# Attention on one core: five eighths of each step's exponentials are kept and exchanged in one round, and V is applied in the step that makes them

## The chip, the core and the metric

The kernel runs on one core of a Trainium2 chip. A core has five engines that run side by side, each through its own list of instructions in order: PE multiplies matrices and writes to PSUM (eight banks of 512 f32 columns in each of 128 partitions), DVE works on vectors, ACT computes functions such as exp, POOL works on vectors too but does not reach PSUM, and SP issues DMA transfers. Sixteen DMA engines move data between HBM and SBUF, and within SBUF. The metric is the time on the device in microseconds; lower is better. All times below without a unit are microseconds, lengths of single instructions excepted where ns is given.

## What is computed

Eight sequences of 512 tokens with 512 features go through one layer of attention with 16 heads of 32. The queries and keys get a second, per-sequence term from `cond`, and the input is added to the result. Cut to what matters:

```python
Q, K, V = (split_heads(x @ W.T + b) for W, b in ((Wq, bq), (Wk, bk), (Wv, bv)))
cQ = Q + split_heads(cond @ Wq.T + bq)
cK = K + split_heads(cond @ Wk.T + bk)
attn = softmax(cQ @ cK.T / sqrt(32))
return x + (attn @ V)
```

Everything is f32.

## The kernel before

**Tasks and steps.** A task `t` is one sequence and one group of four heads: 8 sequences times 4 groups make `T` = 32 tasks. 512 queries and 512 keys are cut into four chunks of 128 each. A step `t` of the main loop (line 1086) mixes the work of several tasks so that every engine has something to do. It has four items, `i` = 0 to 3. Each item holds row scores for one query chunk of task t+1 (in the last item, of t+2), and either a third of a product that makes q, k or v of the next sequence ("P"), or the application of V ("V"). Some items start with a burst of scores as well. The products go by a scheme with seven block products instead of eight (`product`, line 446): a "first" part with 28 matmuls and an "other" part with 28.

**Row scores** (`row_max`, line 578). PE computes for each of the four heads 128 queries against 512 keys (`row_scores`, L607), queries on partitions. DVE takes each row's maximum with its sign turned (`one_max`, L574, for one head; `row_max_of`, L616, for two in neighbouring banks). ACT then computes exp(score - maximum) of the whole row and its sum in one instruction (`denominators`, L654). In most tasks, those in `KEPT` = 2 to 27, the exponentials of the first two query chunks are kept in SBUF; of the other two only the sums are used and the exponentials are written back to PSUM and lost.

**Why an exchange.** To apply V, keys have to be on the partitions. DVE can transpose blocks of 32 by 32 (`turn_kept`, L626: four instructions per task with 1,024 elements per partition each). What is left is to swap whole blocks between the four bands of 32 partitions. `swap_kept` (L640) does this in place with 18 DMA transfers of 128 KB: `move` 0 copies six blocks aside, `move` 1 copies six across, both on SP's queue; `move` 2, on POOL's queue in item 2 of the next step, copies the six from aside. Three rooms for kept exponentials rotate, and V is applied to task t-1 in step t (line 1123 or 1126).

**Bursts.** For the query chunks that are not kept the scores are computed a second time with keys on partitions (`exponentials_of_rest`, line 721): a bf16 matmul over three rows puts the maxima, split into three bf16 parts and transposed by DMA (`split_max` on POOL, `turn_max` L680 on SP), into PSUM (L727); the scores are added (L738); ACT takes exp (L748). There are two bursts of 256 queries per kept step, in items 2 and 3. Tasks outside `KEPT` recompute all 512 (L706, L709, L719).

**Applying V** (`weighted`, line 817). 16 matmuls on the exponentials of the burst, four small ones that spread the sums (L804), 16 on the kept ones (L769). DVE takes reciprocals (L814) and transposes the result (L840), POOL multiplies (L841) and adds the input (L842), and SP stores it in four pieces (L845).

**Making q, k, v.** The "first" parts go from PSUM by two ACT copies (L520, L521) and two POOL additions (L523, L524). The "other" parts of q and k go by three DVE instructions (`other_products`: L536, L481 twice), those of v by two ACT copies (L559, L560) and three POOL additions (`other_by_others`: L561 to L563).

**PSUM.** `order` keeps the eight banks in the order in which they come free; `begin` hands an item eight or (without a burst, "alone") four of them for its row scores, `released` puts them back.

**The order of work** is written out by hand: the program order of each engine is the order of the calls. `TURNED` says after which item's row scores the transposes of the next task stand. After the loop comes a tail for the last tasks (from line 1208), where V is applied in parts between crossed scores of two tasks (`part_of`, `crossed`).

Of the kernel before, what the change touches and what calls it, by code (L numbers as in the profile page):

```python
# [17 lines left out]
def kernel(  # L18
# [14 lines left out]

# [14 lines left out]
    KEPT = range(2, T - 4)  # L71
    KQ = NS // 2
# [5 lines left out]
    qkp = ctx.enter_context(tc.tile_pool(name="qkp", bufs=3))  # L78
    op = ctx.enter_context(tc.tile_pool(name="op", bufs=2))
# [124 lines left out]
    store = EB.tile([P, 18, 2, S], F32, tag="eb", name="store")  # L204

    def room(t):

        at = (t - KEPT[0]) % 3 * 4
        return store[:, at : at + 4].rearrange("p g c (h s) -> p g c h s", s=P)

    ring_at = [0]

    def chunk():

        ring_at[0] += 1
        return store[:, 8 + (ring_at[0] - 1) % 10]

    early = store[:, :8].rearrange("p c i s -> p (c i) s")
# [172 lines left out]
    def pair_of(t, n):  # L391

        if (n, t // 2) not in pairs:
            pairs[n, t // 2] = qkp.tile([P, 2, S], F32, tag=n, name=f"{n}T_{t // 2}")
        return pairs[n, t // 2]
# [25 lines left out]

# [52 lines left out]

    def plus(n, b, u, g, o, pt, rest):

        if n == "v":
            nc.vector.tensor_tensor(o, pt, rest, ALU.add)
        else:
            add = tok[:, "qk".index(n), u * 2 + g, b : b + 1]  # L480
            nc.vector.scalar_tensor_tensor(o, pt, add, rest, ALU.add, ALU.add)  # L481
# [21 lines left out]

    def first_by_others(n, b, u, dens, at, last, mixed):
# [7 lines left out]
        if mixed:  # L512
            dens((0, 1))
            nc.scalar.copy(c2, one_)
# [3 lines left out]
        else:  # L518
            dens()
            nc.scalar.copy(c2, one_)  # L520
# [5 lines left out]
    def other_products(n, b, u, dens, small, at, bias=False):  # L526
# [15 lines left out]
        if n != "v":  # L542
            for g in range(2):
                qkT[n, b * G + u * 2 + g] = pair_of(b * G + u * 2, n)[:, g, :]
# [3 lines left out]
    def other_by_others(n, b, u, dens, small, at):  # L548

        dens()  # L550
# [7 lines left out]
        m45, m23 = aside[:, 0], aside[:, 1]  # L558
        nc.scalar.copy(m45, halves(one_))  # L559
        nc.scalar.copy(m23, halves(two_))  # L560
        nc.gpsimd.tensor_tensor(c12, m45[:, 1, :], c12, ALU.add)  # L561
        nc.gpsimd.tensor_tensor(c2, m45, twice(c22), ALU.add)
        nc.gpsimd.tensor_tensor(c1, m23, c1, ALU.add)  # L563
# [14 lines left out]
    def row_max(t, qc, hold=False, w=HG):  # L578
# [14 lines left out]
        def held():  # L593
            if apart or hold and t < T - 2:
# [25 lines left out]
    kept = {}  # L620

    def turn_kept(t, n):

        pr = slice(n % NP * 2, n % NP * 2 + 2)
        e = kept[t][:, :, n // NP, pr, :].rearrange("p g h s -> p g (h s)")
        nc.vector.transpose(e, e)  # L626

    APART = [(a, g) for a in range(HG) for g in range(a + 1, HG)]
    between = store[:, 16:18]

    def swap_kept(t, move):

        def part(a, g):
            return kept[t][a * BL : (a + 1) * BL, g].rearrange("p c h s -> p (c h s)")

        for n, (a, g) in enumerate(APART):
            at = (n + 2) % HG * BL
            aside = between[at : at + BL, n // HG].rearrange("p i s -> p (i s)")
            to, of = [(aside, part(a, g)), (part(a, g), part(g, a)), (part(g, a), aside)][move]
            (nc.gpsimd if move == 2 else nc.sync).dma_start(to, of)  # L640

    def denominators(t, qc, w=HG, js=range(HG)):
# [3 lines left out]
        keep = t in KEPT and qc < KQ  # L646
        if keep and t not in kept:
            kept[t] = room(t)
        for j in js:
            of = to = banks(w + j)  # L650
            if keep:
                to = kept[t][:, :, qc, j, :].rearrange("p g (c e) -> p g c e", e=BL)
# [8 lines left out]

    def split_max(t, on=nc.gpsimd):
# [3 lines left out]
        m, sp = nmax[t], split[t % 2]  # L666
        rest = op.tile([P, NS, HG, 1], F32, tag="rest", name=f"rest_{t}")
# [7 lines left out]
    def turn_max(t):  # L675

        if t >= T:
# [3 lines left out]
            maxT[t].rearrange("p (c q) -> p c q", c=NS),  # L681
            split[t % 2].rearrange("p c h e -> p (c h e)"),
# [37 lines left out]

    def exponentials_of_rest(t, half):

        bank = [banks(i) for i in range(HG)]
        rest = slice(KQ * P, S)
        for j in range(HG):
            r = slice(j * HD, j * HD + 3)
            nc.tensor.matmul(  # L727
                bank[j],
                onesb[r, :],
                maxT[t][r, rest].unsqueeze(1).broadcast_to([3, 2, HS]),  # L730
# [3 lines left out]
        for i in range(2):  # L734
            kc = half * 2 + i
            for j in range(HG):
                r = slice(j * HD, (j + 1) * HD)
                nc.tensor.matmul(  # L738
                    bank[j][:, i * HS : (i + 1) * HS],
# [5 lines left out]
        for pr in range(NP):  # L745
            e = es[t, half, pr] = store[:, 12 + half * 2 + pr]
            for i in range(2):
                nc.scalar.activation(e[:, i, :], bank[pr * 2 + i], AF.Exp)  # L748
# [12 lines left out]
    def times_v_half(t, kc, half, pt):  # L761
        b, g = divmod(t, G)
        for j in range(HG):
            if half:
                at = kc % 2 * HS
                e = es[t, kc // 2, j // 2][:, j % 2, at : at + HS]
            else:
                e = kept[t][:, :, :, j, kc * BL : (kc + 1) * BL].rearrange("p a c e -> p c a e")
            nc.tensor.matmul(  # L769
                pt[j * HD : (j + 1) * HD, half * HS : (half + 1) * HS],  # L770
                vs[b % 2][:, kc, (g * HG + j) * HD : (g * HG + j + 1) * HD],
                e,
                start=(kc == 0),
                stop=(kc == NS - 1),
# [42 lines left out]
    def weighted(t, pt, pd, between):  # L817

        apart = masked(t)
        if t in KEPT:
            for kc in range(NS):
                times_v_half(t, kc, 1, pt)
            spread_sums(apart, pd)
            for kc in range(NS):
                times_v_half(t, kc, 0, pt)
# [7 lines left out]
        send(t, pt, rec)  # L835
# [526 lines left out]
```

## Time and profile before

| | us |
|---|---|
| Runs (median of 3) | 670.43 (669.88, 670.43, 675.13) |
| The profiled execution | 668.33 |
| Its span, first to last instruction | 666.5 |
| Mean granted clock of PE | 0.999 of full speed |

In the profile a line starts with the source line (L607 is line 607) and the engine; `psum<-kT,qT` names what is written and read; `x1024` counts records. An f32 matmul leaves two records in the trace, so `x8` stands for four matmuls. `PEld` are weight loads, which overlap PE. In a group's line the first numbers are the busy time in all and the mean length of one in ns, and behind the second bar stands how long the engine idled before them and what ended most of it. In a timeline the first number is the start, the second the length. The figure "us to landing" is from the issue of a DMA to its arrival.

### The profile page before, as it was taken

How to read it: one execution, taken by the hardware profiler on the slowest of the kernel's cores; microseconds unless marked ns; L12 is line 12 of the kernel's file. 1: busy time of each engine (PE TensorE's matmuls, PEld its weight loads, DVE VectorE, ACT ScalarE, POOL GpSimd, SP SyncE). 2: the span in 40 equal slices, each digit the busy share in tenths (PEclk: the TensorE clock that was granted, in tenths of full speed). 3: DMA queues.
4: the chain of work that ended last, by engine and by line, in shares of the span. 5: the costliest groups of instructions: out<-in, count | busy, mean ns of one | idle time of the engine just before them, and what ended most of it. 6: DMA issues, size and time to landing. Idle time of an engine off the chain costs nothing.

```text
span 666.5 us, 24514 instructions
## 1 busy us (share of the span) xinstructions
PE 659.8 (99%) x9784; PEld 339.6 (51%) x9784; DVE 561.7 (84%) x752; ACT 557.4 (84%) x1396; POOL 407.1 (61%) x577
## 2 busy tenths in 40 slices
PE   9999999999999999999999999999999999999997
PEld 8444444555555555555555555555555555555432
DVE  3798898889988888998888989888898988766877
ACT  2479889888889988888988888898888889888664
POOL 3641326677666875768566785668765776663261
PEclk9999999999999999999999999999999999999999
DMA  7723238897889888878888888787887687671111
GB/s 188 110 41 58 35 58 181 170 184 164 159 162 181 164 186 186 179 157 176 168 176 174 179 176 168 167 185 152 164 182 153 149 181 159 145 163 23 26 32 32
DMA packets 245862, 94.90 MB, mean 142 GB/s; under 512 B 229099, under 2 KB 229611, under 8 KB 245749
## 3 DMA queue, kind: packets, MB, share of 16 engines
q1 hardware_dynamic: 236500, 71.83, 56.4%
q0 software_dynamic: 7488, 20.46, 10.9%
q8 instruction: 77, 1.26, 0.8%
q10 hardware_dynamic: 1760, 1.05, 0.5%
q14 instruction: 37, 0.29, 0.2%
HBM read 19.75 MB, written 8.39 MB: 42 GB/s over the span
## 4 chain that ended last, share of the span: by engine, by line
PE 96%; DMA 1%; DVE 1%; POOL 1%; issue 0%; DVEq 0%; POOLq 0%
PE psum L456 43%; PE psum L607 19%; PE psum L769 14%; PE psum L738 6%; PE psum L753 3%; PE psum L727 2%; PE psum L709 2%; PE psum L399 2%; PE psum L706 1%; PE psum L1186 1%; PE psum L779 1%; DMA w_q<-in_L_cond_Wq_dram 1%; DMA maxT<-split 0%; PE psum L308 0%; POOL store L640 0%; PE psum L353 0%
## 5 line engine op out<-in xcount | busy, mean ns | idle before, releaser
L574 DVE TENSOR_REDUCE nmax<-psum 128x1 f32<-128x512 f32 x246 | 158.2, 685 | 71.8 <-PE psum L607 70.3
L654 ACT ACTIVATE psum<-psum,nmax 128x512 f32<-128x512 f32 x272 | 180.4, 670 | 16.6 <-DVE nmax L616 8.7
L616 DVE TENSOR_REDUCE nmax<-psum 128x2 f32<-128x1024 f32 x127 | 154.1, 1214 | 1.3 <-PE psum L607 1.3
L654 ACT ACTIVATE store<-psum,nmax 128x512 f32<-128x512 f32 x208 | 141.7, 692 | 11.4 <-DVE nmax L616 6.7
L607 PE MATMUL psum<-kT,qT 32*128 32x512 f32 x1024 | 149.7, 620 | 0.2 <-DVE kT L481 0.2
L748 ACT ACTIVATE store<-psum 128x512 f32<-128x512 f32 x208 | 107.4, 604 | 34.7 <-PE psum L738 34.7
L626 DVE STREAM_TRANSPOSE store<-store 128x1024 f32<-128x1024 f32 x104 | 127.5, 1226 | 0.0
L769 PE MATMUL psum<-store,v 128*32 128x256 f32 x1664 | 96.8, 381 | 0.0
L640 POOL DMA_DIRECT2D store<-store x156 | 77.5, 501 | 27.5 <-DMA store<-store 13.7
L769 PEld LDWEIGHTS psum<-store,v 128*32 128x32 f32 x1664 | 48.9, 110 | 46.5 <-ACT store L654 16.7
L607 PEld LDWEIGHTS psum<-kT,qT 32*128 32x128 f32 x1024 | 51.0, 183 | 39.4 <-issue 23.0
L841 POOL TENSOR_TENSOR res<-res,recs 128x512 f32<-128x512 f32 x30 | 31.4, 1048 | 42.3 <-DVE res L840 42.3
L654 ACT ACTIVATION_READ_ACCUMULATOR psum<-psum,nmax 128x1 f32 x272 | 57.1, 210 | 0.0
L738 PE MATMUL psum<-qT,kT 32*128 32x256 f32 x832 | 53.7, 374 | 0.0
L201 POOL TENSOR_TENSOR xr<-xr,bvs 128x512 f32<-128x512 f32 x30 | 38.5, 1285 | 15.1 <-DMA xr<-in_x_dram 15.0
L456 PE MATMUL psum<-wc_v,xc 128*32 128x256 f32 x768 | 47.7, 379 | 0.0
L719 ACT ACTIVATE store<-psum 128x512 f32<-128x512 f32 x72 | 37.2, 605 | 12.2 <-PE psum L709 9.0
L456 PE MATMUL psum<-xc,wc_q 128*32 128x256 f32 x720 | 44.5, 379 | 0.0
L456 PE MATMUL psum<-xc,wc_k 128*32 128x256 f32 x720 | 44.5, 379 | 0.0
L654 ACT ACTIVATION_READ_ACCUMULATOR store<-psum,nmax 128x1 f32 x208 | 43.1, 207 | 0.0
L738 PEld LDWEIGHTS psum<-qT,kT 32*128 32x128 f32 x832 | 40.8, 184 | 3.3
L842 POOL TENSOR_TENSOR res<-res,xr 128x512 f32<-128x512 f32 x30 | 38.5, 1285 | 2.4
(193 smaller groups left out, 1017.7 us busy)
## 6 DMA issues: line engine op xcount, KB each, us to landing
store<-store SPq DMA_DIRECT2D x312, 128.0 KB, 2.3
store<-store POOLq DMA_DIRECT2D x156, 128.0 KB, 3.6
out_dram<-res SPq DMA_DIRECT2D x122, 64.0 KB, 3.8
xr<-in_x_dram SPq DMA_DIRECT2D x120, 64.0 KB, 2.6
x<-in_x_dram SPq DMA_DIRECT2D x112, 64.0 KB, 2.9
w_q<-in_L_cond_Wq_dram SPq DMA_DIRECT2D x4, 256.0 KB, 3.8
w_v<-in_L_cond_Wv_dram SPq DMA_DIRECT2D x16, 64.0 KB, 2.6
w_k<-in_L_cond_Wk_dram SPq DMA_DIRECT2D x16, 48.0 KB, 2.5
```

Of the source, the lines that this page charges most:

```text
L201: nc.gpsimd.tensor_tensor(xr[t], xr[t], bias, ALU.add)
L456: nc.tensor.matmul(pt[r], still[:, r], moving, start=(kc == kcs[0]), stop=(kc == kcs[-1]))
L574: nc.vector.tensor_reduce(nmax[t][:, qc, j : j + 1, 0], pt, AX.X, ALU.max, negate=True)
L607: nc.tensor.matmul(pt, qkT["q", t][r, qc * P : (qc + 1) * P], qkT["k", t][r, :], start=True, stop=True,)
L616: nc.vector.tensor_reduce(nmax[t][:, qc, pr * 2 : pr * 2 + 2, 0], pt, AX.X, ALU.max, negate=True)
L626: nc.vector.transpose(e, e)
L640: (nc.gpsimd if move == 2 else nc.sync).dma_start(to, of)
L654: nc.scalar.activation(to, of, AF.Exp, bias=nmax[t][:, qc, j, :], accum_out=sums[t][:, qc, j, :],)
L738: nc.tensor.matmul(bank[j][:, i * HS : (i + 1) * HS], qkT["k", t][r, kc * P : (kc + 1) * P], qkT["q", t][r, rest], start=False, stop=(i == 1),
L748: nc.scalar.activation(e[:, i, :], bank[pr * 2 + i], AF.Exp)
L769: nc.tensor.matmul(pt[j * HD : (j + 1) * HD, half * HS : (half + 1) * HS], vs[b % 2][:, kc, (g * HG + j) * HD : (g * HG + j + 1) * HD], e, ...
L842: nc.gpsimd.tensor_tensor(y, y, xr.pop(t), ALU.add)
```

## The change

1. **More is kept.** Of a kept task's exponentials, query chunks 0 and 1 are kept for all keys and chunk 2 for key chunks 0 and 1 (`FULL`, `HALF`): five eighths. So the burst for key chunks 0 and 1 covers only query chunk 3 (128 queries), the one for key chunks 2 and 3 covers 256 as before. The bursts stand in items 0 (the narrow one) and 2. The row chunks are taken in the order 1, 3, 2, 0 (`IN_TURN`), because chunk 2 is written in full and chunk 0 then covers its surplus. Only the maxima of chunks 2 and 3 are split and transposed. `KEPT` reaches to 28.
2. **One round.** `meet` copies all 16 blocks (160 KB each, those that stay in their band too) from the task's room (two rooms now) into a room of its own, `MET`: 12 transfers on SP in item 0, four on POOL in item 1. `swap_kept` is gone. A fifth `turn_kept` per task is needed (`UNITS`); of the five one or more stand in the step in which they are exchanged.
3. **V in the same step.** A kept step's items are "P", "P", "P", "V", and `weighted` works on task t itself. It writes two banks, so the result is transposed in two halves; POOL's multiplication and addition and the stores follow in the next step, after `meet` (`unsent`). Step 1 applies V twice, to tasks 0 and 1, and the tail no longer applies V to task 28.
4. **Work moves from DVE to ACT and POOL.** The "other" parts of q and k go by one ACT copy, one DVE addition of the bias and three POOL additions; the "first" parts of q and k leave by a copy and a copy with bias of half the size each, and a full copy. The "other" part of v of the second half goes by DVE. In item 1 of a kept step the row maxima are four single reductions.

```diff
-    KEPT = range(2, T - 4)
-    KQ = NS // 2
+    KEPT = range(2, T - 3)
+    FULL = 2
+    HALF = 2
+    IN_TURN = (1, 3, HALF, 0)
...
-    store = EB.tile([P, 18, 2, S], F32, tag="eb", name="store")
+    PAD = HS
+    BLOCK = FULL * S + HS
+    ROOM = HG * BLOCK
+    ROOMS = (0, ROOM + PAD)
+    REST = 2 * (ROOM + PAD)
+    MET = REST + 6 * S
+    store = EB.tile([P, MET + ROOM], F32, tag="eb", name="store")
...
+    UNITS = [(S, 0), (S, 1), (FULL * S, None), (0, 0), (0, 1)]
...
+    def meet(t, ns, queue):
+        for n in ns:
+            a, g = n % HG, (n + n // HG) % HG
+            of, to = room(t) + g * BLOCK, MET + a * BLOCK
+            queue.dma_start(
+                store[g * BL : (g + 1) * BL, to : to + BLOCK],
+                store[a * BL : (a + 1) * BL, of : of + BLOCK],
+            )
...
+    def rest_at(kc):
+        return slice((FULL if kc >= HALF else FULL + 1) * P, S)
+
     def exponentials_of_rest(t, half):
+        kcs = [(2, 3), (0, 1)][half]
+        rest = rest_at(kcs[0])
+        n = S - rest.start
...
-            for kc in range(NS):
-                times_v_half(t, kc, 1, pt)
+            for kc in (2, 3, 0, 1):
+                times_v_rest(t, kc, pt[1], kc == 2, False)
             spread_sums(apart, pd)
             for kc in range(NS):
-                times_v_half(t, kc, 0, pt)
+                times_v_kept(t, kc, pt[0], range(FULL), kc == 0, kc == NS - 1)
+            for kc in range(HALF):
+                times_v_kept(t, kc, pt[1], [FULL], False, kc == HALF - 1)
...
-        return [(s, i - 2)] if i >= 2 else []
+        return [(s, 1 - i // 2)] if i % 2 == 0 else []
...
+    OTHERS = "kq"
+    MEET = (range(12), range(12, 16))
+    TURNED = {(0, 0): 1, (0, 1): 1, (2, 0): 1, (2, 1): 1, (2, 2): 1}
+    TURNED_1 = {(0, 0): 1, (0, 1): 2, (2, 0): 1, (3, 1): 1}
...
-        items = "PVPP" if t - 1 in KEPT else "VPPP"
+        items = ["P", "P", "P", "V"] if t in KEPT else ["V", "P", "P", "PV"]
...
+            if t in KEPT and i == 0:
+                while todo[t]:
+                    turn_kept(t, len(UNITS) - todo[t])
+                    todo[t] -= 1
+                meet(t, MEET[0], nc.sync)
+            while unsent:
+                unsent.pop()()
+            if t in KEPT and i == 1:
+                meet(t, MEET[1], nc.gpsimd)
+            if i == (1 if t + 1 in KEPT else 2):
                 split_max(t + 1)
                 turn_max(t + 1)
```

More of the change, by code (lines that the diff above doesn't have):

```diff
@@ L645, in denominators @@
             return
-        keep = t in KEPT and qc < KQ
-        if keep and t not in kept:
-            kept[t] = room(t)
+        keep = t in KEPT and qc <= FULL
         for j in js:
@@ L651, in denominators @@
             if keep:
-                to = kept[t][:, :, qc, j, :].rearrange("p g (c e) -> p g c e", e=BL)
+                to = of_room(room(t), qc, j, range(NS))
                 of = of.rearrange("p (c g e) -> p g c e", g=HG, e=BL)
@@ L733, in exponentials_of_rest @@
             )
-        for i in range(2):
-            kc = half * 2 + i
+        for i, kc in enumerate(kcs):
             for j in range(HG):
```

232 lines of the change are left out of this document (132 added, 100 removed).

## The prediction

> **What bounds the kernel now.** I read the busy line and the chain first, then the windows of four steps of the main loop, then PE's timeline of one step.
>
> ```profile
> span 666.5 us, 24514 instructions
> PE 659.8 (99%) x9784; PEld 339.6 (51%) x9784; DVE 561.7 (84%) x752; ACT 557.4 (84%) x1396; POOL 407.1 (61%) x577
> PE 96%; DMA 1%; DVE 1%; POOL 1%; issue 0%; DVEq 0%; POOLq 0%
> ```
>
> ```profile
> 313.36:333.09 19.73, 19.73 (x316) 10.49 (x313) 17.44 (x23) 17.23 (x45) 11.89 (x19) 1.00 0.79 164
> sum 78.27, PE 78.27 PEld 41.12 DVE 69.48 ACT 69.27 POOL 54.26; mean PE 19.57 PEld 10.28 DVE 17.37 ACT 17.32 POOL 13.56
> ```
>
> The columns are length, then busy time of PE, PEld, DVE, ACT, POOL, then granted clock, DMA share and GB/s. A step lasts 19.57 on the mean of four; PE is busy all of it, DVE 17.37, ACT 17.32, at full clock. A modelled end can hide a short wait of PE, so I take PE's costs from one start to the next:
>
> ```profile
> 313.36 0.39 PE L727 MATMUL psum<-maxT,onesb 3*128 3x512 bf16 x4
> 313.58 1.03 PE L738 MATMUL psum<-qT,kT 32*128 32x256 f32 x16
> 314.45 1.02 PE L607 MATMUL psum<-kT,qT 32*128 32x512 f32 x8
> 315.41 1.07 PE L456 MATMUL psum<-xc,wT_q 128*32 128x256 f32 x16
> ...
> 318.57 0.40 PE L727 MATMUL psum<-maxT,onesb 3*128 3x512 bf16 x4
> ...
> 329.43 1.93 PE L769 MATMUL psum<-store,v 128*32 128x256 f32 x32
> 331.19 0.23 PE L804 MATMUL psum<-apart,modulo 128*32 128x16 f32 x8
> 331.25 1.91 PE L769 MATMUL psum<-store,v 128*32 128x256 f32 x32
> 333.09 0.40 PE L727 MATMUL psum<-maxT,onesb 3*128 3x512 bf16 x4
> ```
>
> An f32 matmul is two records. A burst of recomputed scores costs 0.22 for its bf16 maxima and 0.87 for the rest: 1.09. The item around it lasts 5.21 (313.36 to 318.57). Applying V costs 3.66 (329.43 to 333.09). So the question is what the change takes from PE, and whether another engine then makes PE wait.
>
> **PE, the scores.** A kept step has two bursts of half its queries. In the changed kernel the burst for key chunks 0 and 1 covers one query chunk: 16 records of 128 columns and four bf16 matmuls of 256. If cost goes with columns it is 0.11 + 0.435 = 0.545, and 0.545 is saved. The trace has no 32-row matmul of 128 columns; the weights may be what is left, since their size does not shrink. The nearest rows:
>
> ```profile
> 661.54 0.60 PE L849 MATMUL psum<-ident,store 128*128 128x128 f32 x4
> 661.98 0.38 PE L1311 MATMUL psum<-ident,store 128*128 128x128 f32 x2
> L738 PEld LDWEIGHTS psum<-qT,kT 32*128 32x128 f32 x832 | 40.8, 184 | 3.3
> ```
>
> Four f32 loads and matmuls of 128 by 128 start 0.44 apart, 0.11 each. A row group runs four records of the narrow burst one after another: 4 x 0.11 = 0.44, as by columns. The other bound takes the load's whole 184 ns: 0.74 + 0.11 = 0.85, and 0.24 is saved. I take 0.545, by L849, which does both things in its 0.11. The Trainium skill ("TensorE: Matmul & The Clock Gate", The mechanism) says that a weight load overlaps running matmuls only where their row groups differ. With the 107 ns for 128 columns of its section LDWEIGHTS, a narrow record would take 107 + 107 ns and the burst would save 0.12, an estimate; but the wide burst's four rounds in 0.87 leave no room for such a load beside the columns, so the trace disagrees.
>
> Steps 2 to 27 gain this: 26 x 0.545 = 14.2. Step 28 becomes a kept step. It now runs from its first burst to the tail's:
>
> ```profile
> 597.24 0.40 PE L706 MATMUL psum<-maxT,onesb 3*128 3x512 bf16 x4
> ...
> 619.28 0.40 PE L706 MATMUL psum<-maxT,onesb 3*128 3x512 bf16 x4
> ```
>
> That is 22.04, against 19.57 - 0.545 = 19.0: 3.0 saved. Applying V streams as many columns as before in 80 records instead of 64; eight records of 16 columns pass in 0.06 (331.19 to 331.25), so short ones cost no more than their columns, and I count nothing.
>
> **The tail.** V of task 28 moves from the tail into the loop, and V of task 1 from step 2 into step 1: PE's 3.66 moves, and the tail gets 3.66 shorter if PE alone bounds it. But there:
>
> ```profile
> 624.52 2.06 ACT L1201 ACTIVATE store<-psum 128x512 f32<-128x512 f32 x4 [0.55 <-PE psum L1186]
> ...
> 627.71 2.06 ACT L1201 ACTIVATE store<-psum 128x512 f32<-128x512 f32 x4 [0.63 <-PE psum L1186]
> ```
>
> Each turn is 3.19, of which 2.06 are exponentials that empty the banks and about 1 is V's filler. Without it PE waits for banks. Bounds: nothing lost, 3.66 lost; I take 1.5.
>
> **DVE.** It becomes the engine next to PE:
>
> ```profile
> L574 DVE TENSOR_REDUCE nmax<-psum 128x1 f32<-128x512 f32 x246 | 158.2, 685 | 71.8 <-PE psum L607 70.3
> L616 DVE TENSOR_REDUCE nmax<-psum 128x2 f32<-128x1024 f32 x127 | 154.1, 1214 | 1.3 <-PE psum L607 1.3
> L626 DVE STREAM_TRANSPOSE store<-store 128x1024 f32<-128x1024 f32 x104 | 127.5, 1226 | 0.0
> L536 DVE TENSOR_TENSOR qT<-psum,qT 128x256 f32<-128x256 f32 x15 | 6.2, 412 | 0.0
> L481 DVE SCALAR_TENSOR_TENSOR qT<-psum,tok,qT 128x512 f32<-128x512 f32 x29 | 20.5, 740 | 0.2 <-PE psum L727 0.2
> L412 DVE TENSOR_SCALAR qT<-psum,tok 128x512 f32<-128x512 f32 x2 | 1.5, 750 | 0.8 <-PE psum L399 0.8
> ```
>
> Per step: a fifth transpose, +1.23; two single reductions for one double, 1.37 - 1.21 = +0.16; the result's transpose in two, +0.1 (bounds 0 and one more 0.7). One "other" product of q or k per step loses 0.41 + 2 x 0.74 = 1.89 and keeps one of 0.75; one V product in four steps comes back, about 1.89 / 4 = 0.47. Sum 17.37 + 1.23 + 0.16 + 0.1 - 1.89 + 0.75 + 0.47 = 18.2 of 19.0. So it fits, but unevenly. In three steps of four the item of the full burst carries two transposes behind its maxima. Its maxima start 1.09 + 1.05 into the item (L574 began 1.05 after L607 at 314.45: see DVE's rows below, 315.50), take 2.58 and end at 4.72; two transposes end at 7.2, or 2.0 into the next item, where maxima could start at 1.05. The lag is 0.95, or about 0.5 as neighbours on DVE overlap. The last two exponentials of those scores free banks for the next step's first row scores:
>
> ```profile
> 328.36 1.14 PE L607 MATMUL psum<-kT,qT 32*128 32x512 f32 x8
> L654 ACT ACTIVATE store<-psum,nmax 128x512 f32<-128x512 f32 x208 | 141.7, 692 | 11.4 <-DVE nmax L616 6.7
> ```
>
> Without lag they end at 1.05 + 2.58 + 2 x 0.69 = 5.0 in the item of V; PE asks for the banks at 4.73 (328.36 to 333.09) + 0.55 = 5.28. So the lag less 0.28, 0.2 to 0.7, may show as a wait in three steps of four, or nothing. I take the low end, 0.15 on the mean of steps: 27 x 0.15 = 4.
>
> ```profile
> 313.49 0.72 DVE L840 STREAM_TRANSPOSE res<-psum 128x512 f32<-128x512 f32 x1
> 314.13 1.20 DVE L626 STREAM_TRANSPOSE store<-store 128x1024 f32<-128x1024 f32 x1
> 315.50 0.69 DVE L574 TENSOR_REDUCE nmax<-psum 128x1 f32<-128x512 f32 x1 [0.17 <-PE psum L607]
> ```
>
> **ACT and POOL** stay below PE. ACT loses half of four rest exponentials (604 ns each to about 400: -0.8) and gains about 0.5 in copies of q and k: near 17. POOL drops two DMA issues of 0.49 and gains three additions for each "other" product of q and k, less one V product in four steps:
>
> ```profile
> L748 ACT ACTIVATE store<-psum 128x512 f32<-128x512 f32 x208 | 107.4, 604 | 34.7 <-PE psum L738 34.7
> L494 ACT COPY v<-psum 128x256 f32<-128x256 f32 x2 | 0.8, 407 | 0.0
> L523 POOL TENSOR_TENSOR qT<-qT 128x512 f32<-128x512 f32 x13 | 16.7, 1285 | 9.6 <-ACT qT L521 9.6
> L524 POOL TENSOR_TENSOR qT<-qT 128x256 f32<-128x256 f32 x14 | 10.2, 732 | 4.6 <-DVE qT L516 3.6
> ```
>
> 13.56 - 0.98 + 3.30 - 0.82 = 15.1 of 19.0. If that cover went, k would reach the next batch's row scores late; at an item's distance it does not.
>
> **The exchange.** It used to have almost a step; now V waits for it in its own step.
>
> ```profile
> 307.43 8.65 SPq L640 DMA_DIRECT2D store<-store  x12
> L640 SPq DMA_DIRECT2D store<-store x312: 507/545/1876, 91.1 to 587.0; - x156
> DMA to landing us min/median/max: 2.1/3.1/5.8
> maxT<-split SPq DMA_TRANSPOSE x29, 3.4
> ```
>
> The fifth transpose stands first in the next step, so the transfers may start about 2.0 after the previous V ended (L626 above: 314.13 + 1.20, V having ended at 313.36). SP issues twelve in 6.5 (545 ns each) to 8.65; the last lands 2.3 to 5.8 later: at 10.8 to 16.5. POOL's four stand behind its additions for that item's product, which ends near 4.7: some 2.0 of additions and 2.0 of issues bring the last to 9 to 10, landed by 16. The kept part of V starts 19.0 - 2.3 = 16.7 after the previous V. So it is covered, by 0.2 at the worst pairing. Behind the twelve on SP stand four result stores and the transposed maxima that the next narrow burst needs: 10.65 + 4 x 0.65 + 3.4 = 16.7, before 19.0. Each transfer is a quarter larger; if that lengthens the issue too, 8.65 x 1.25 = 10.8, and the maxima land at 18.8. If the cover is gone, PE waits by what is missing, each step.
>
> **Sum.** 668.33, the profiled execution, of which 666.5 is the span: 668.33 - 14.2 - 3.0 + 1.5 + 4 = 656.6. The median of the runs lies 2.1 above (670.43, runs 669.88 to 675.13): 658.7.
>
> **The rivals.**
> Weights bound the narrow burst: it saves 0.24 and not 0.545, 26 x 0.305 = 8 more, 667. For it: the 184 ns in each load's row. Against: L849.
> DVE becomes the bound, and the kernel slower. Its maxima wait for PE (70.3 of 71.8 idle in L574's row), its result transposes for V's end, and both stand in line before the transposes. Now it idles 19.57 - 17.37 = 2.2 per step. If that idle stays, a step is 18.2 + 2.2 = 20.4: 26 x 0.83 = 22 more, less 1.6 in step 28, plus 1.5: median 692. It decides from an idle of 1.4 on (19.57 - 18.2). At 0.8 it costs nothing. Against: much of the idle was waiting that work can fill.
> The exchange comes late: at 5.8 for each last landing and one more issue delay of 2, V waits 1.8 a step: +48, median 703. Against: the landings have a median of 3.1.
> PE gains without any wait, and the tail fully: 668.33 - 17.2 + 2.1 = 653.2; this is the low end of my forecast.
>
> **Chances.** PE-bound with small waits, 652 to 664: 0.66. Weights: 0.10. DVE: 0.13, half of it at partial idle, 664 to 678. Exchange: 0.05. The rest, 0.06, is what the rows don't show, such as strided transposes or exponentials that cost more. A range of 651 to 676 leaves about 2 in 10 out. About 1% is what a measurement can tell from no change: faster, below 663.7, takes the forecast and little else, 0.67; within, 0.17; slower, above 677.1, 0.16.
>
> **What would show it.** Right: V-end to V-end about 19.0 to 19.2, narrow burst near 0.55, DVE busy 18.2, transfers landed before V's kept part. Wrong: PE waiting for DVE or ACT at the row scores, a narrow burst of 0.85, or V idle for a transfer.

## The result and the profile after

The changed kernel takes 694.96 us (median of 4 runs, 692.08 to 696.87), the kernel before 671.83 in the same comparison: a ratio of 1.034 [1.028, 1.040], so 3.4% slower where 2% faster was forecast. The profiled execution took 696.87, its span is 695.0.

The page of the changed kernel: span, busy line, chain by engine and by line.

```profile
span 695.0 us, 25350 instructions
PE 653.9 (94%) x10240; PEld 355.0 (51%) x10240; DVE 583.4 (84%) x798; ACT 535.7 (77%) x1428; POOL 446.5 (64%) x591
PE 41%; DMA 17%; SPq 12%; POOL 10%; ACT 8%; DVE 8%; issue 3%; DVEq 0%; POOLq 0%; ACTq 0%
PE psum L452 15%; SPq L650 9%; PE psum L621 8%; DMA store<-store 6%; DMA out_dram<-res 5%; PE psum L789 5%; ACT psum L665 4%; DMA maxT<-split 4%; DVE store L643 3%; POOL store L650 3%; PE psum L776 2%; DVE nmax L588 2%; PE psum L396 2%; PE psum L759 2%; ACT store L665 2%
```

PE has 6 us less work than before (653.9 against 659.8), as it should, but 41 us in which it does nothing, against 7. The chain, which was PE for 96%, is PE for 41% and DMA with SP's queue (SPq) for 29%: the transfers of `meet` (L650) are what the end waits for. PE's timeline shows where in a step:

```profile
314.14 1.14 PE L621 MATMUL psum<-kT,qT 32*128 32x512 f32 x8
315.21 1.51 PE L801 MATMUL psum<-store,v 128*32 128x256 f32 x32
316.54 0.23 PE L836 MATMUL psum<-apart,modulo 128*32 128x16 f32 x8
318.67 2.37 PE L789 MATMUL psum<-store,v 128*32 128x256 f32 x48 [1.90 <-DMA out_dram<-res]
320.97 0.29 PE L749 MATMUL psum<-maxT,onesb 3*128 3x256 bf16 x4
321.09 0.62 PE L759 MATMUL psum<-qT,kT 32*128 32x128 f32 x16
321.54 1.19 PE L621 MATMUL psum<-kT,qT 32*128 32x512 f32 x8
```

The narrow burst is as forecast, 0.57 from 320.97 to 321.54. The kept part of V (L789) stands 1.90 idle. In the program it waits for all 16 transfers; the result's stores behind them land in the same microseconds, and the profile names the one that landed last (`out_dram<-res`). The two groups that wait for the transfers, from the page (behind the second bar: idle time before them, and what ended most of it), and the transfers themselves, from the view of their line:

```profile
L665 ACT ACTIVATE store<-psum,nmax 128x512 f32<-128x512 f32 x324 | 220.4, 696 | 63.2 <-DMA out_dram<-res 27.5
L789 PE MATMUL psum<-store,v 128*32 128x256 f32 (+1 forms) x1296 | 67.4, 358 | 24.3 <-DMA out_dram<-res 13.9
```

```profile
L650 SPq DMA_DIRECT2D store<-store x324: 507/592/1892, 98.4 to 633.2; - x162
DMA to landing us min/median/max: 2.4/4.6/8.0
```

Before, the transfers landed after 2.1/3.1/5.8. ACT waits as PE does: with two rooms its row exponentials for task t+2 overwrite the room that the transfers of task t still read. And SP itself is late. Its queue in the same step, and the chain through it:

```profile
298.47 2.17 SPq L149 DMA_DIRECT2D x<-in_x_dram  x2
300.68 2.08 SPq L167 DMA_DIRECT2D xr<-in_x_dram  x4
302.92 10.41 SPq L650 DMA_DIRECT2D store<-store  x12
313.43 3.23 SPq L886 DMA_DIRECT2D out_dram<-res  x4
316.75 1.80 SPq L696 DMA_TRANSPOSE maxT<-split  x1
318.66 2.12 SPq L149 DMA_DIRECT2D x<-in_x_dram  x4
320.82 2.81 SPq L167 DMA_DIRECT2D xr<-in_x_dram  x4
323.79 2.42 SPq L650 DMA_DIRECT2D store<-store  x4
```

```profile
by line: SPq L650 43.6%; DMA out_dram<-res 19.4%; SPq L149 8.2%; PE psum L789 7.6%; SPq L167 7.5%; issue 4.7%; DVE store L643 4.3%; DVE res L877 3.4%; ACT psum L665 3.0%; DVE nmax L588 2.4%; SPq L886 0.1%
...
309.52 1.28 SPq L650
...
310.84 1.64 SPq L650
```

V had ended at 299.7 and the fifth transpose at 301.4, yet the first transfer goes out at 302.92, behind the loads of x and xr. Some issues take 1.28 or 1.64 and not 0.59. In the built program each DMA on SP waits for the landing of the eighth before it, but that is not what makes these long: the eighth before the one at 309.52 went out at 303.49 and had landed at 306.95. Of SP's 137 issues of over 0.7 in the kept steps (the transposed maxima aside) the trace has that landing for 78, and in all 78 it came before the issue began. What does make them long is open. They come with the exchange: SP issues for 18.4 of a step's 20.3, and in the kernel without transfers (run 1 below) for 7.3; the DMAs other than the transfers take 9.6 of a step against those 7.3. So the long issues delay the loads behind them, and the loads delay the transfers of the next step (323.79, where V ended at 320.97).

A wait can also cost PE its clock; in this run one did so twice. Behind a wait of 4.07 the kept part of V at 112.88 takes 3.99, and behind one of 2.08 that at 440.93 takes 3.97, where 2.30 is usual, both at a mean granted clock of 0.57. Not every wait does it: behind the 1.90 shown above the clock is 1.00. First and third of these, with the columns as in the prediction (length, busy time of PE, PEld, DVE, ACT, POOL, granted clock, DMA share, GB/s):

```profile
112.88:116.87 3.99, 3.99 (x49) 2.64 (x50) 0.45 (x1) 2.73 (x8) 0.00 (x0) 0.57 0.65 101
318.67:320.97 2.30, 2.30 (x49) 1.63 (x50) 0.66 (x3) 2.30 (x7) 2.12 (x2) 1.00 0.49 81
```

### The profile page after: what moved, and what is told of

Same layout as the page of the kernel before. It is cut to its first block, busy times and chain, and to the rows that moved or that the text cites. A ratio compares the mean times of both kernels' runs of the same rounds, so it can differ in the third digit from the quotient of the medians.

```text
span 695.0 us, 25350 instructions
## 1 busy us (share of the span) xinstructions
PE 653.9 (94%) x10240; PEld 355.0 (51%) x10240; DVE 583.4 (84%) x798; ACT 535.7 (77%) x1428; POOL 446.5 (64%) x591
## 3 DMA queue, kind: packets, MB, share of 16 engines
q0 software_dynamic: 5184, 17.70, 10.2%
## 4 chain that ended last, share of the span: by engine, by line
PE 41%; DMA 17%; SPq 12%; POOL 10%; ACT 8%; DVE 8%; issue 3%; DVEq 0%; POOLq 0%; ACTq 0%
PE psum L452 15%; SPq L650 9%; PE psum L621 8%; DMA store<-store 6%; DMA out_dram<-res 5%; PE psum L789 5%; ACT psum L665 4%; DMA maxT<-split 4%; DVE store L643 3%; POOL store L650 3%; PE psum L776 2%; DVE nmax L588 2%; PE psum L396 2%; PE psum L759 2%; ACT store L665 2%
## 5 line engine op out<-in xcount | busy, mean ns | idle before, releaser
L665 ACT ACTIVATE store<-psum,nmax 128x512 f32<-128x512 f32 x324 | 220.4, 696 | 63.2 <-DMA out_dram<-res 27.5
L588 DVE TENSOR_REDUCE nmax<-psum 128x1 f32<-128x512 f32 x296 | 187.1, 681 | 28.9 <-PE psum L621 28.5
L643 DVE STREAM_TRANSPOSE store<-store 128x1024 f32<-128x1024 f32 x135 | 163.0, 1222 | 0.5 <-ACT store L665 0.5
L630 DVE TENSOR_REDUCE nmax<-psum 128x2 f32<-128x1024 f32 x102 | 123.7, 1214 | 2.3 <-PE psum L621 2.3
L665 ACT ACTIVATE psum<-psum,nmax 128x512 f32<-128x512 f32 x156 | 103.5, 667 | 15.4 <-DVE nmax L588 14.3
L771 ACT ACTIVATE store<-psum 128x256 f32<-128x256 f32 (+1 forms) x216 | 88.5, 497 | 29.0 <-PE psum L759 28.6
L789 PE MATMUL psum<-store,v 128*32 128x256 f32 (+1 forms) x1296 | 67.4, 358 | 24.3 <-DMA out_dram<-res 13.9
L665 ACT ACTIVATION_READ_ACCUMULATOR store<-psum,nmax 128x1 f32 x324 | 69.2, 214 | 0.0
L789 PEld LDWEIGHTS psum<-store,v 128*32 128x32 f32 x1296 | 46.6, 113 | 40.4 <-issue 27.6
L650 POOL DMA_DIRECT2D store<-store x108 | 54.1, 506 | 0.0
L180 POOL TENSOR_TENSOR xr<-xr,bvs 128x512 f32<-128x512 f32 x30 | 38.4, 1278 | 10.1 <-DMA xr<-in_x_dram 10.0
L759 PE MATMUL psum<-qT,kT 32*128 32x128 f32 (+1 forms) x864 | 44.6, 322 | 0.0
L534 POOL TENSOR_TENSOR qT<-qT 128x512 f32<-128x512 f32 x13 | 16.7, 1284 | 40.5 <-ACT qT L532 40.5
L801 PE MATMUL psum<-store,v 128*32 128x256 f32 (+1 forms) x864 | 40.7, 329 | 0.0
```

The source lines that it names most:

```text
L180: nc.gpsimd.tensor_tensor(xr[t], xr[t], bias, ALU.add)
L588: nc.vector.tensor_reduce(nmax[t][:, qc, j : j + 1, 0], pt, AX.X, ALU.max, negate=True)
L630: nc.vector.tensor_reduce(nmax[t][:, qc, pr * 2 : pr * 2 + 2, 0], pt, AX.X, ALU.max, negate=True)
L650: queue.dma_start(store[g * BL : (g + 1) * BL, to : to + BLOCK], store[a * BL : (a + 1) * BL, of : of + BLOCK],)
L665: nc.scalar.activation(to, of, AF.Exp, bias=nmax[t][:, qc, j, :], accum_out=sums[t][:, qc, j, :],)
L759: nc.tensor.matmul(bank[j][:, i * n : (i + 1) * n], qkT["k", t][r, kc * P : (kc + 1) * P], qkT["q", t][r, rest], start=False, stop=(i == 1),)
```

## The experiments

Theory A: what came late is the exchange, and all else of the prediction holds; after the first four runs it became C: the exchange lasts 13 to 14 us because of its bytes, and what V waits is decided by when it starts. The rivals: other engines bound the kernel (B), the bytes alone decide (A1), SP's queue of eight alone decides (A2, D), the DMA ports of the two halves of the partitions (E). All kernels are the changed kernel with the edit shown. In the table, the ratio is to the kernel before in the same comparison (its medians are 669.94 to 672.10), step is the mean of 26 kept steps, from the start of one kept part of V to the next; the first transfer on SP and the last landing of the 16 count from the end of the previous V, means too, worked out from the issues and landings that the trace has (over a third of the landings of SP's transfers are missing, in all runs alike, so the last one is at times later than shown). Without any wait the kept part of V starts at 16.95.

| kernel | median | ratio to before | step | first on SP | last landing |
|---|---|---|---|---|---|
| the changed kernel | 694.96 | 1.034 [1.028, 1.040] | 20.33 | 2.98 | 16.8 |
| 1 no exchange | 660.46 | 0.984 [0.980, 0.988] | 19.25 | - | - |
| 2 half the bytes | 668.53 | 0.997 [0.995, 0.999] | 19.31 | 3.94 | 14.0 |
| 3 no loads | 701.72 | 1.045 [1.040, 1.049] | 20.51 | 3.63 | 17.3 |
| 4 V on other data | 690.73 | 1.032 [1.025, 1.039] | 20.15 | 3.35 | 17.2 |
| 5 exchange alone on SP | 676.68 | 1.005 [1.001, 1.008] | 19.85 | 1.83 | 16.8 |
| 6 POOL's four first | 672.91 | 1.001 [0.998, 1.005] | 19.45 | 2.74 | 15.7 |
| 7 xr on POOL's queue | 689.86 | 1.025 [1.018, 1.032] | 20.23 | 2.25 | 16.9 |
| 8 sources alternate | 685.10 | 1.019 [1.013, 1.024] | 19.87 | 2.90 | 16.3 |
| 9 = 6 and 8 | 668.78 | 0.995 [0.992, 0.997] | 19.33 | 2.41 | 15.0 |
| 10 = 9, stores on POOL | 677.56 | 1.007 [1.005, 1.010] | 19.86 | 1.83 | 15.5 |
| 11 = 9, xr on POOL | 665.86 | 0.990 [0.987, 0.993] | 19.34 | 1.85 | 15.6 |
| 12 sources sorted | 716.41 | 1.064 [1.060, 1.068] | 21.00 | 3.27 | 17.6 |
| 13 targets sorted | 707.17 | 1.054 [1.052, 1.057] | 20.68 | 2.78 | 17.5 |
| 14 ten and six | 684.97 | 1.020 [1.016, 1.025] | 20.00 | 2.65 | 16.9 |

**1. No exchange.**

```diff
-        for n in ns:
+        for n in ():
```

> Leaves out all 16 transfers of a step; V works on what lies in MET. Theory A (what came late is the exchange; every other term of the prediction holds): V never waits, a step is 19.2 to 19.4, time 652 to 662. Rival B (DVE, ACT or POOL bound the changed kernel even without the exchange): 680 or more, PE waiting at the row scores.

660.46, step 19.25. PE's timeline, with V and the burst behind it, and PE's longest wait of the run (in all, times, longest):

```profile
318.81 1.14 PE L621 MATMUL psum<-kT,qT 32*128 32x512 f32 x8
319.88 1.51 PE L801 MATMUL psum<-store,v 128*32 128x256 f32 x32
321.20 0.23 PE L836 MATMUL psum<-apart,modulo 128*32 128x16 f32 x8
321.26 2.35 PE L789 MATMUL psum<-store,v 128*32 128x256 f32 x48
323.54 0.29 PE L749 MATMUL psum<-maxT,onesb 3*128 3x256 bf16 x4
```

```profile
PE psum L621 <- DVE nmax L630: 1.3, 1, 1.3
```

V costs 3.66 (319.88 to 323.54), as before. PE's longest wait in the whole run is 1.3, once, in the tail. B falls. What the exchange costs is 695.0 - 658.9 = 36.1 of span.

**2. Half the bytes.**

```diff
-                store[g * BL : (g + 1) * BL, to : to + BLOCK],
-                store[a * BL : (a + 1) * BL, of : of + BLOCK],
+                store[g * BL : (g + 1) * BL, to : to + BLOCK // 2],
+                store[a * BL : (a + 1) * BL, of : of + BLOCK // 2],
```

> All 16 transfers stay, each with 640 of its 1,280 columns; the rest of MET keeps old data. If the bytes of the exchange bound it (A1): transfers land within 3 to 4 us, V waits no more, 654 to 665. If the number of transfers on SP's queue bounds it, each of the 25 there waiting for the eighth before it (A2): landings shorten too, but the issue of twelve keeps its 7 to 9 us, so the gain is partial, 665 to 685. B: no change from 695.

668.53, and V does not wait in any step, though SP's first transfer goes out at 3.94, a microsecond later than in the changed kernel. From first issue to last landing the exchange takes 10.1 instead of 13.8. The number of transfers and the queue of eight are the same, so the bytes are a main part: of 13.8, some 7.5 go with them (twice 13.82 - 10.05) and 6.3 do not, an estimate that takes the length as linear in the bytes. By its time the run falls into A2's range and not A1's; but its steps, 19.31, are nearly those without the exchange, and what is left stands behind the last kept V: 52.2 to the end against 46.7, most of it POOL's closing (below).

**3. No loads.**

```diff
+            if n >= 6:
+                xs[n] = xs[n - 2]
+                return
             xs[n] = xp.tile([P, NB, BL], F32, tag="x", name=f"x_{n}")
...
-            for h in range(HG):
-                nc.sync.dma_start(
-                    xr[t][h * BL : (h + 1) * BL], spread(x[b], g * P + h * BL)
-                )
...
-        nc.gpsimd.tensor_tensor(xr[t], xr[t], bias, ALU.add)
+        nc.gpsimd.tensor_tensor(
+            xr[t], xs[5] if turned_by_vector(t) else xr[t], bias, ALU.add
+        )
```

> Leaves out the eight loads of x and xr per step from SP's queue; products and residuals use old blocks, every other operation stays. A2 (SP reaches the exchange late because the loads stand before it, and these stand behind the last transfers): the first transfer is issued at 1.7 us after V's end in every step, 655 to 668. A1 (bytes of the exchange itself): the loads are only 0.5 of 3.4 MB a step, so 682 to 692. B: 695.

701.72, slower, which no theory had. SP's timeline says why: in the built program the first of the result's stores, which waits for POOL, now stands before the transfers.

```profile
346.70 0.32 SPq L887 DMA_DIRECT2D out_dram<-res  x1
347.19 10.15 SPq L651 DMA_DIRECT2D store<-store  x12
357.39 3.07 SPq L887 DMA_DIRECT2D out_dram<-res  x3
```

So the edit did not do what it was for, and does not settle A2. It shows something else: with no loads at all and a start at 3.63 the exchange still takes 13.7.

**4. V on other data.**

```diff
-                at_store(MET + cs[0] * S + kc * P + j * BL, (S, n), (BLOCK, HG), (1, BL)),
+                wT["q"][:, :n, :].rearrange("p n (a e) -> p n a e", a=HG)[:, :, :, j * BL : (j + 1) * BL],
```

> The exchange stays whole, but the kept part of V reads a weight tile in place of MET, so PE no longer waits for the transfers. If only PE's wait at the kept part costs time: 655 to 665. If ACT's wait to write the room that the transfers still read costs as well (63 us idle before the row exponentials): PE stalls at the row scores instead, 670 to 690. B: 695.

690.73: taking away PE's wait at V gains 4 of 695. The waits of PE and of ACT:

```profile
PE psum L749 <- DMA maxT<-split: 18.3, 12, 3.1
```

```profile
ACT store L665 <- DMA out_dram<-res: 15.1, 11, 2.8
ACT store L665 <- DMA store<-store: 10.6, 5, 4.4
```

PE now waits behind V, for the transposed maxima, which stand behind the transfers on SP, and ACT waits for the room as before. Part of the gain is lost again to the clock: PE is granted 0.50 in four stretches of 3.4 here, in two in the changed kernel. The exchange bounds the step from three sides.

**5. The exchange alone on SP.** As 3, and the stores on POOL's queue:

```diff
-                nc.sync.dma_start(spread(out[b], g * P + h * BL), y[h * BL : (h + 1) * BL])
+                nc.gpsimd.dma_start(spread(out[b], g * P + h * BL), y[h * BL : (h + 1) * BL])
```

> Leaves out the loads of x and xr (old blocks are used) and puts the result's four stores on POOL's queue, so that SP has only the twelve transfers and the transposed maxima of a step. In the run without loads one store stood before the transfers and they started at 3.4 us after V's end; here nothing stands before them. Theory C (the transfers last 12.5 to 14.5 us from first issue to last landing because of their bytes, and what V waits is decided by when they start): first issue at 1.7 in every step, last landing by 16.3, V waits under 0.4 a step, 660 to 670. Rival A1 (bytes alone; an earlier start only queues them longer): landings stay at 17 to 18, 683 to 700.

676.68, between the two ranges. The start is at 1.83 in every step, but the last landing stays at 16.8: the start was 1.1 earlier and the exchange 1.1 longer, 14.9 from first issue to last landing. So the exchange doesn't keep its length whenever it starts, as C has it. A step falls to 19.85 all the same; what gave it isn't separated here, since the loads, their bytes and the place of the stores changed together. Some 5 of the gain are another thing, POOL's closing (below).

**6. POOL's four first.**

```diff
                 meet(t, MEET[0], nc.sync)
+                meet(t, MEET[1], nc.gpsimd)
             while unsent:
                 unsent.pop()()
-            if t in KEPT and i == 1:
-                meet(t, MEET[1], nc.gpsimd)
```

> POOL's four transfers go out in item 0 ahead of the result's multiplication, some 6 us earlier, beside SP's first; nothing is left out. C: the DMA engines are not full in the first 6 us (landings of 2.5 to 3.3 there against 5 to 8 later), so the exchange ends 2 to 3 us earlier, V waits little, 662 to 675. A1 (the engines are full already): landings lengthen from the start, the end stays, 685 to 700. D (SP's queue of eight is what makes it long): SP's twelve still end late, 680 to 695.

672.91, 22 less than the changed kernel, with nothing left out: C's range, below those of A1 and D, though SP keeps its 25 DMAs a step. The kept part of V, from the view by line:

```profile
L789 PE MATMUL psum<-store,v 128*32 128x256 f32 (+1 forms) x1296 | 64.0, 345 | 3.0 <-DMA out_dram<-res 1.5 <-DMA maxT<-split 0.7 <-DMA store<-store 0.6
```

Its idle time falls from 24.3 to 3.0. The engines had room in the first 6 us of the exchange, when only SP issued: with POOL's four among them SP's first four now land after 4.5 to 6.2 (medians; 2.5 to 3.1 in the changed kernel) and its last four after 3.8 to 4.4 (4.8 to 5.7), and the last landing comes 1.1 earlier. This also shows that the two queues share engines.

**7. xr on POOL's queue.**

```diff
-                nc.sync.dma_start(
+                nc.gpsimd.dma_start(
                     xr[t][h * BL : (h + 1) * BL], spread(x[b], g * P + h * BL)
                 )
```

> The four loads of xr go on POOL's queue instead of SP's; nothing is left out. C: xr was what kept SP until 1.7 to 4.8 after V's end; now the first transfer goes at 1.7 to 2.0 in every step, 665 to 678; POOL has 2 us more and may take some of it back. A1: 688 to 697. D: as C.

689.86, in A1's range, but this hides two opposite things. In the first 22 of the 26 steps SP's first transfer goes out at 1.85 instead of 3.19, and a step takes 19.77 instead of 20.48: of the 1.22 above the 19.26 of the kernel without exchange, an early start takes 0.71 (0.08 of it is the clock, at half for 3.4 twice in those steps of the changed kernel and once here). The last four steps, in which no x is loaded any more, take 22.78 instead of 19.52: there a store stands before the transfers again, as SP's timeline shows for the worst of them, of 24.25, with V ended at 551.1. Of the 13.0 that these four steps take more than in the changed kernel, some 5 are PE at half clock behind the waits (granted 0.50 from 572.0 to 578.8 and from 616.4 to 623.2, PE busy for 10.4 of the 13.6).

```profile
557.90 0.32 SPq L886 DMA_DIRECT2D out_dram<-res  x1
558.38 10.43 SPq L650 DMA_DIRECT2D store<-store  x12
```

The changed kernel itself says the same: in its own last four steps, with half of the loads gone, SP starts at 1.83 and a step takes 19.52. A start at 1.8 doesn't suffice, though: a step is still 0.5 too long.

**8, 12 and 13. The order of the 16 transfers.** Each moves a band of 32 partitions to a band of 32. Sources alternating between the halves of the partitions (8), sorted by half (12), and alternating sources with sorted targets (13):

```diff
-            a, g = n % HG, (n + n // HG) % HG
+            a = (0, 2, 1, 3)[n % HG]              # 8
+            g = (a + n // HG) % HG
...
+            a = n % 2 + n // 8 * 2                # 12
+            g = (a + n // 2 % 4) % HG
...
+            a, g = (0, 2, 1, 3)[n % HG], n // HG  # 13
```

> Only the order of the 16 transfers: source bands 0, 2, 1, 3 in place of 0, 1, 2, 3, so that neighbours in the queue read from different halves of the 128 partitions. E (a band of 32 partitions reaches only half of the ports, and two neighbours on the same half share them): landings shorten by 1 us or more, 670 to 685. C and A1: 690 to 698, no change.

> The changed kernel with another order of the 16 transfers: sources in the bands 0 and 1 first (eight), then those in 2 and 3 (four on SP and POOL's four at the same time). E (neighbours that read from one half of the partitions share its ports): landings longer than in the changed kernel, 700 to 720. C without ports: 692 to 698.

> The changed kernel with the sources alternating between the halves (bands 0, 2, 1, 3) as in the run of 685, but sorted by target: four into band 0, four into band 1, four into band 2 on SP, four into band 3 on POOL, so that SP's first eight all write into one half. If the ports bind on the reading side alone: 683 to 688, as that run. If writing binds as reading does: 700 to 716, as the run with the sources sorted. Both sides partly: 690 to 700.

685.10, 716.41 and 707.17 against 694.96, by the order alone. The idle time before the kept part of V, from the view by line, 8 first, then 12 and 13:

```profile
L790 PE MATMUL psum<-store,v 128*32 128x256 f32 (+1 forms) x1296 | 65.3, 350 | 12.8 <-DMA out_dram<-res 6.1 <-DMA store<-store 3.5 <-DMA maxT<-split 2.8
```

```profile
L790 PE MATMUL psum<-store,v 128*32 128x256 f32 (+1 forms) x1296 | 67.3, 357 | 32.4 <-DMA out_dram<-res 22.4 <-DMA store<-store 8.4 <-issue 1.5
```

```profile
L789 PE MATMUL psum<-store,v 128*32 128x256 f32 (+1 forms) x1296 | 66.6, 355 | 34.0 <-DMA out_dram<-res 20.8 <-DMA store<-store 12.5 <-issue 0.6
```

From first issue to last landing the exchange takes 13.4, 14.3 and 14.8. The order counts, as E has it, and the targets' order counts by itself: 8 and 13 have the same order of sources. For the sources by themselves no run tells, since in 8 the targets alternate nearly as well and in 12 they too come in runs of up to four of one half. And 13 sorts the targets by band as well as by half, so that it is the half and not the band isn't shown for writing; in 12 neighbours read from different bands of one half.

**9, 10 and 11. Together.** 6 and 8 together (9), then also the stores (10) or the loads of xr (11) on POOL's queue, by the lines shown.

> POOL's four transfers ahead of its result work and source bands in the order 0, 2, 1, 3 together; nothing is left out. If the two gains come from different causes (an early start of the four; ports of both halves) the exchange ends by 15 us after V's end at the latest, no step waits, a step is 19.25 to 19.35 and the span is 501 + 5 for the longer closing above the run without exchange: 664 to 668. If halves only helped because they eased the same queue: 670 to 674.

> As the run before it in this call, and the result's four stores go on POOL's queue, straight behind the instruction that makes the result. SP has 21 transfers a step in place of 25, POOL 2 us more work. C: SP's first transfer goes at 1.7 to 1.9 in every step. The closing of POOL (10.2 us in the changed kernel, 4.3 in the kernels with 120 more transfers on its queue) shrinks by 5. Together 658 to 665. If POOL's two extra microseconds delay k and v: PE waits at the row scores or products, 665 to 675.

> As the first run of this call, and the four loads of xr on POOL's queue, where they stand in front of the four transfers. C: SP starts at 1.7 in every step; POOL's four start some 2 us later than without. 660 to 668, the shorter closing included. If late steps of the loop, where no x is loaded and a store can stand before the transfers, dominate: 668 to 678.

9 takes 668.78, a microsecond above its window. The first kept V waits 0.6 and no later one more than 0.42, though the last landing, 15.0 on the mean, comes at up to 16.6. 10, with 677.56, goes beyond even the bad branch of its expectation, since POOL is late with k:

```profile
PE psum L621 <- POOL kT L576: 11.7, 12, 1.8
```

The changed kernel also has two tiles for k where there were three (`kp`, two buffers), which the list of changes leaves out; whether this counts here was not tried.

11 takes 665.86, 1% less than the kernel before ([0.987, 0.993] of it), and is the best of those that leave nothing out. Its page:

```profile
span 663.3 us, 25376 instructions
PE 651.4 (98%) x10240; PEld 354.2 (53%) x10240; DVE 582.8 (88%) x798; ACT 537.2 (81%) x1428; POOL 525.3 (79%) x715
```

PE is the bound again. Its span is 4.4 above the kernel without exchange: this is all that the exchange still costs, POOL's longer closing (below) included.

**14. Ten and six.**

```diff
-    MEET = (range(12), range(12, 16))
+    MEET = (range(10), range(10, 16))
```

> The changed kernel with ten of the transfers on SP and six on POOL (162 on POOL's queue in all, against 108). If the closing of POOL depends on how many transfers its queue had (10.2 us with 108, 4.3 with 156 in the kernel before): it takes 4 to 5 us here; otherwise 10.2. The exchange: SP's part ends earlier, POOL's two more start at 11 to 12 us and land at 17 to 18, so the time stays near 690 to 697, less 5 if the closing is shorter.

684.97 (two runs, 682.55 and 687.38), just below its window; the exchange lands as late as before, and POOL's closing is short. Its length in ns stands as the third number of the row, from the view of the last line: in the changed kernel (108 transfers on POOL's queue), the kernel before (156), this one (162), 11 (232) and 1 (none).

```profile
L1416 POOLq DRAIN  x3: 34/102/10216, 684.0 to 694.7; - x3
```

```profile
L1357 POOLq DRAIN  x3: 34/102/4249, 660.6 to 666.3; - x3
```

```profile
L1416 POOLq DRAIN  x3: 34/102/4736, 674.7 to 680.5; - x3
```

```profile
L1416 POOLq DRAIN  x3: 40/102/4580, 657.3 to 663.0; - x3
```

```profile
L1416 POOLq DRAIN  x3: 34/82/1374, 652.4 to 658.7; - x3
```

## Why the prediction was wrong

**The step that failed** is the exchange: "the last lands 2.3 to 5.8 later: at 10.8 to 16.5 ... So it is covered, by 0.2 at the worst pairing." It lands at 16.8 on the mean and at up to 18.6, where the kept V could start at 16.95. Three things went into it wrongly. The landing times were those of 128 KB transfers; of 160 KB they have a median of 4.6 and a maximum of 8.0. The start "about 2.0 after the previous V ended" was taken from the transpose; SP reached it at 1.8 to 4.9, since the loads stand before it on a queue whose issues had grown longer (18.4 us of a step's 20.3). And POOL's four were put at 9 to 10 and "landed by 16", as if two queues did not share the engines: they went out at 8.5 to 11.1, and from then on SP's landings have medians of 4.7 to 5.7, against 2.5 to 3.2 of its first six. A cover of 0.2, with the bounds of another transfer size, was no cover. The rival "the exchange comes late" named the mechanism, with 1.8 a step and a chance of 0.05; it measured 1.1 a step, 20.33 against 19.25, and should have been the likeliest case. (Its 703 is 658.7 + 48 less the 4 taken for DVE's lag, which the rival doesn't say.)

The 36.1 of span between the kernel without exchange and the changed one, from the records: the first kept V starts 3.4 later, 26 steps take 528.6 against 500.5, so 28.1, and from the end of the last kept V to the end it is 51.2 against 46.7, so 4.5. The last is the closing of POOL, 10.2 against 1.4 (of the 8.8 more, 4.5 show, since the rest of the closing ends later than POOL's 1.4), which no term of the sum had. Of the 28.1, PE idles 20.2 before the kept V and 3.4 before the narrow burst, for the transposed maxima; some 3.4 more is the half clock, 1.7 each time. That the transfers cause the 28.1 is shown by 1, 2 and 6. Of the 1.22 a step in the first 22 steps an early start took 0.71, by 7, in which POOL's work changes too; that the 0.5 left is the length of the exchange itself is argued and not shown. The two are no independent parts: 9 removes nearly all of both without touching the loads (19.33).

**What held.** The narrow burst costs 0.57 for the 0.545 worked out, so the rival of the weights (0.85) is out. The Trainium skill's rule ("TensorE: Matmul & The Clock Gate", The mechanism), that a load overlaps only where row groups differ, would have saved 0.12 a burst by the estimate set beside it; 1.09 - 0.57 = 0.52 was saved, so the measurement stands against that sentence here. V in 80 records costs 3.66, nothing more. Step 28 falls from 22.04 to 19.14, as the 3.0 said. In the kernel without exchange the windows of its main loop, 109.43 to 612.24, give DVE, ACT and POOL:

```profile
109.43:612.24 502.81, 502.81 (x8595) 273.19 (x8585) 464.26 (x615) 434.99 (x1182) 336.89 (x409) 1.00 0.27 44
```

At 19.25 of 502.81 a step that is 17.8 for DVE (18.2 forecast), 16.7 for ACT (17), and 12.9 for POOL, 14.9 with the four issues (15.1). DVE as the bound (692) is out, though the time of the changed kernel would have fitted it, by luck: only the waits and the run without the exchange tell the two apart. The 0.15 a step for DVE's lag can't be told from the trace: PE shows no wait in these steps, and a modelled end can hide a short one.

**What was off in size.** Without the exchange the span is 658.9, where the sum gives 656.6 - 1.8 = 654.8. The tail is one part: 619.28 to 666.5 is 47.2 before, with V of task 28 in it, and 46.7 in the kernel without the exchange, without. Of V's 3.66 only 0.5 was saved, so 3.1 are lost where 1.5 was taken; the upper bound was the better value. (Up to PE's last matmul 1.1 was saved; what follows it took 0.6 more.) Of the rest, some 2.5, about 2 are steps of 19.25 where 19.57 - 0.545 + 0.15 = 19.18 was the sum; the remainder is open.

## What to carry to other kernels

A transfer that has just enough time is a risk to be priced on the far side: take its landing from transfers of its own size, in the company that it will have on the engines, and ask what stands before it on its queue when everything runs late. When a burst of transfers is the bound, start all queues at its beginning and let neighbours alternate between the halves of the partitions, at both ends, before cutting bytes. And take the transfers out once: the time that is left tells whether the rest of a prediction holds.

## What the runs showed of the hardware

- **The order of the bands.** Sixteen transfers of 160 KB from 32 partitions to 32 take 13.4 from first issue to last landing when their sources, and nearly always their targets, alternate between the halves, 14.3 to 14.8 when sources or targets are sorted. The Trainium skill ("SBUF — State Buffer", Door 1: The DMA port swizzle) says that the partitions 0 to 63 reach eight of the sixteen DMA ports and 64 to 127 the other eight; the runs fit this, though none shows a port. The same page (section "Can I just issue two DMAs to hit both halves?") has two concurrent transfers, one in each half, at only 6% over a single one. That is another comparison than the one here, of orders of the same sixteen; here sorting makes the exchange 7 to 10% longer. At the edge of a wait this became 31 us of the kernel, 685.10 to 716.41.
- **Shared engines.** Where only SP issued, its transfers landed after 2.5 to 3.2 (medians of the first six); with POOL's four among them the medians are 4.7 to 5.7, and the longest took 8.0. Moving the four to the beginning brought the last landing from 16.8 to 15.7 with the same bytes.
- **The closing of POOL** took 1.4 us without a transfer on its queue, 4.0 to 4.7 with 156, 162, 228 or 232, and 10.2 with 108, in every kernel that had 108. What else it depends on was not tried.
